# Cross-attention on one core: a new order for the first slots and for the end

## The chip, the core and the metric

The kernel runs on one core of a Trainium2 chip. A core has a matrix engine (TensorE, PE in the profile; its weight loads are listed as PEld), a vector engine (VectorE, DVE), a scalar engine (ScalarE, ACT), GpSimd (POOL) and a queue engine that mostly issues DMAs (SyncE, SP). Matmul results land in PSUM, which has eight banks of 128 x 512 floats. The metric is the device time of one execution in microseconds; lower is better.

## The reference

All inputs are fp32. `x` is 32 x 512 x 640, the context 32 x 77 x 1024. There are 20 heads of 32 columns. Only the first 77 context rows exist, so the three further attention branches of the reference have no keys and add nothing. What remains is

```python
q = heads(x @ to_q_w)                      # 32 x 20 x 512 x 32
k = heads(ctx @ to_k_w)                    # 32 x 20 x  77 x 32
v = heads(ctx @ to_v_w)
s = einsum('bhqd,bhkd->bhqk', q, k) / sqrt(32)
p = softmax(s, axis=-1)
h = merge(einsum('bhqk,bhkd->bhqd', p, v))
out = h @ to_out_w + to_out_b + x
```

## The kernel before

**Precision.** A product with weights is made of three matmuls: both operands are split into a rounded high half and the rest, and high x high, high x low and low x high are summed in PSUM (`PAIRS`). Scores and values are plain fp32 matmuls.

**First stage.** Keys and values of all 32 batches are computed from the transposed context in five groups of columns (`keys`, `values_of`) and stored to two scratch tensors in DRAM. The values of the last group (`LAST`) are not finished there: their five blocks, 24 matmuls each, are done by `context_values` next to the first attention work. After the matmuls of a block, `split_values` transposes it out of PSUM on VectorE (`vs`, L210) and GpSimd issues four stores of it (L216).

**Slots.** The rest is 160 slots, n = 5 b + j: batch b and chunk j of 128 columns, that is four heads (`HPC`) with 512 queries. Every instruction stream is in program order; there is no scheduler that reorders it. Slot n does the following, each step on its own engine:

- `scores(n)`: 16 small matmuls per query tile and head into four PSUM banks, one for each head (`sc`, four buffers). They read the query copy `qt` of this slot.
- `maxima(n)`: four reductions on VectorE, one for each bank (L430).
- `transpose_p(n - 1)`: VectorE transposes the normalized probabilities of the slot before into `z` (L459), and `move_p(n - 1)` lets four DMAs gather `z` into `raw` (L468, two buffers).
- `exps(n, i)`: ScalarE takes the exponentials of the four banks with row sums (L440); the first writes the probability tile of this slot.
- `queries(n + 1)`: 15 matmuls into the bank `pq` (L401). `copy_q(n + 1)` copies it to `qt` (L410), on VectorE as long as there is no output work, later on ScalarE.
- `values(n - 3)`: four matmuls into the bank `pa` (L478), from `raw`. `high_a` (ScalarE, L492) and `low_a` (VectorE, L497) split the result into `at`. There is one `pa` bank, so the next values wait for `low_a`.
- `normalize(n)`: a reciprocal on VectorE (L450), then GpSimd multiplies the probabilities (L452).
- `piece(...)`: 12 to 18 matmuls of an output projection (L515) of an earlier batch, in one of two output banks (`po`). `finish` adds a completed half tile to the residual tile `xr` (L544), which frees the bank, and stores the tile when both halves are there. `add_bias` adds the bias to a residual tile on GpSimd (L508).
- The x of a coming batch is loaded, transposed in four parts on VectorE (`transpose_x`, L235) and split (`split_x`, ScalarE L245 and GpSimd L246).

In slots 0 to 6 no batch is ready for its output projection (`has_out` is false). Slots 0 and 1 carry the last context blocks instead (`beside`): block 2 in slot 0, blocks 4 and 3 in slot 1. Their PSUM banks are released after slot 1 and become `pa` and the two `po` banks; from there on `po` exists, but is first used in slot 7. The values start in slot 3.

In the slots without output work the steps stand in this order, with the query copy last:

```python
        if ahead:
            queries(n + 1)
        if taken is not None and not has_out:
            values(taken)
        if len(beside) > 0:
            context_values(LAST, beside[0], psv)
        if ahead and not has_out:
            copy_q(n + 1, nc.vector.tensor_copy)
```

**End.** After slot 159, `end` finishes the projection of batch 30 (pieces 6 to 9), does the values of slots 157, 158 and 159 (`take` is values, high half, low half) and projects batch 31. By then the score banks are free, so the eight half tiles of batch 31 are begun in them and in the other banks (`begin`) and closed with the last chunk (`close`).

Of the kernel before, what the change touches and what calls it, by code (L numbers as in the profile page):

```python
# [23 lines left out]
P = 128  # L24
# [13 lines left out]
def kernel(  # L38
# [179 lines left out]
    def context_values(g, j, pool):  # L218
        values_of(g, j, pool)
        split_values(g, j)  # L220
# [12 lines left out]
    def transpose_x(b, i):  # L233
        part = xss[b][:, 4 * i : 4 * i + 4, :].rearrange("p a u -> p (a u)")
        nc.vector.transpose(part, part)  # L235
# [173 lines left out]
    def copy_q(n, copy=nc.scalar.copy):  # L409
        copy(qts[n % 2], pqs.pop(n))  # L410

    def scores(n):
        b, j = divmod(n, NC_)
        scs[n] = [ps.tile([P, NQ, P], F32, tag="sc", name="sc", bufs=4) for _ in range(HPC)]
        for t in range(NQ):
            for i, sc in enumerate(scs[n]):
                r = slice(i * HD, (i + 1) * HD)
                nc.tensor.matmul(  # L418
                    sc[:, t, :NKEY],
                    qts[n % 2][r, t * P : (t + 1) * P],  # L420
                    kbs[b % 2][r, j, :],
                    start=True,
                    stop=True,
                    tile_position=(i * HD, 0),
                )

    def maxima(n):
        nms[n] = main.tile([P, HPC, NQ], F32, tag="nm", name="nm", bufs=2)
        for i, sc in enumerate(scs[n]):
            nc.vector.tensor_reduce(  # L430
                nms[n][:, i], sc[:, :, :NKEY], AX.X, ALU.max, negate=True
            )
# [23 lines left out]
    def transpose_p(n):  # L456

        pn, z = pnb[n % 2], zs[n % 2]
        nc.vector.transpose(  # L459
            z.rearrange("p c h t j -> p (h t) c j"),  # L460
            pn.rearrange("p a (c i) -> p a c i", i=Q),
        )
# [10 lines left out]
    def values(n):  # L473
        b, j = divmod(n, NC_)
        raw, vb = raws.pop(n), vbs[b % 2][:, j]
        pas[n] = late[1].tile([P, S], F32, tag="pa", name="pa", bufs=1)
        for i in range(HPC):
            nc.tensor.matmul(  # L478
                pas[n][i * HD : (i + 1) * HD, :].rearrange("p (a q) -> p a q", q=P),
                vb[:, i, :],  # L480
                raw[:, :, i, :],
                start=True,
                stop=True,
                tile_position=(0, i * HD),
            )
# [9 lines left out]
    def low_a(n):  # L495
        at = ats[n]
        nc.vector.tensor_tensor(  # L497
            at[:, 1, :], pas.pop(n), at[:, 0, :].bitcast(F32), ALU.subtract
        )

    def load_residual(b, t, xr=None):
        if xr is None:
            xr = late[0].tile([P, C], F32, tag="xr", name="xr", bufs=4)
        nc.sync.dma_start(xr, x[b, t * P : (t + 1) * P, :])
        xrs[b, t] = xr

    def add_bias(b, t):
        nc.gpsimd.tensor_tensor(xrs[b, t], xrs[b, t], bias, ALU.add)  # L508
# [21 lines left out]
    def piece(b, i):  # L530
        for t, h, j in STEPS[CUTS[i] : CUTS[i + 1]]:
            if j == 0:
                output_bank(b, t, h)
            project(b, t, h, j)
            if j == NC_ - 1:
                closed.append((b, t, h))

    def finish():

        while closed:  # L540
            b, t, h = closed.pop(0)
            xr = xrs[b, t]
            cols = slice(h * HALF, (h + 1) * HALF)
            nc.vector.tensor_tensor(  # L544
                xr[:, cols], pos.pop((b, t, h))[:, :HALF], xr[:, cols], ALU.add
            )
            if (b, t) == (B - 1, NQ - 1):
                nc.sync.dma_start(out[b, t * P : (t + 1) * P, cols], xr[:, cols])
            elif h == 1:
                nc.sync.dma_start(out[b, t * P : (t + 1) * P, :], xr)  # L550
# [11 lines left out]
    TRANSPOSE_X = {0: (0, 1), 1: (2, 3)}  # L562
    SPLIT_X = {2: (0, 1), 3: (2, 3, 4)}

    WO = {1: (0, 1, 2), 2: (3,), 3: (4,)}
    wos = []

    def take(m):
        values(m)
        high_a(m)  # L570
        low_a(m)

    def slot(n, beside=()):
        b, j = divmod(n, NC_)
        ahead, more = n + 1 < N, b + 1 < B
        back, first = PIECES[j]
        bo_, has_out = b - back, b >= back
        xsplits = (SPLIT_X if b else {0: (2,), 1: (3,), 2: (4,)}).get(j, ()) if more else ()
        turns = TRANSPOSE_X.get(j, ()) if more and b else ()
        if b == 1 and j < 2:  # L580
            turns = ((), range(NQ))[j]
        taken = takes.get(n)
        scores(n)
        if taken is not None and has_out:
            values(taken)
        maxima(n)
        if n:
            transpose_p(n - 1)
        for k in WO.get(n, ()):
            nc.sync.dma_start(wos[0][:, k].bitcast(F32), wo_dram[:, k].bitcast(F32))  # L590
        if j == 0 and more:
            load_keys(b + 1)
        if j == 1:
            load_values(b)
        if b + 2 < B:
            quarters = {4: (0, 1), 5: (2, 3)}.get(n, ()) if n <= NC_ else (j - 1,) if j else ()
            if quarters:
                load_x(2 if n <= NC_ else b + 2, quarters)
        if j in RESIDUAL and b >= RESIDUAL[j][0]:
            load_residual(b - RESIDUAL[j][0], RESIDUAL[j][1])  # L600
        if j in BIAS and b >= BIAS[j][0]:
            add_bias(b - BIAS[j][0], BIAS[j][1])
        if has_out:
            piece(bo_, first)
        for i in range(2):
            exps(n, i)
        finish()
        if n >= LATE:
            move_p(n - 1)
        for i in turns:  # L610
            transpose_x(b + 1, i)
        if len(beside) > 1:
            context_values(LAST, beside[1], psv)
        if ahead:
            queries(n + 1)
        if taken is not None and not has_out:
            values(taken)
        if len(beside) > 0:
            context_values(LAST, beside[0], psv)
        if ahead and not has_out:  # L620
            copy_q(n + 1, nc.vector.tensor_copy)
        for i in range(2, HPC):
            exps(n, i)
        normalize(n)
        if taken is not None:
            high_a(taken)
        if has_out and ahead:
            copy_q(n + 1)
        if has_out:
            piece(bo_, first + 1)  # L630
        if taken is not None:
            low_a(taken)
        for c in xsplits:
            split_x(b + 1, c)
        finish()

    def end():


        last = B - 1  # L640
        transpose_p(N - 1)
        add_bias(last - 1, 3)
        piece(last - 1, 6)
        finish()
        load_residual(last, 0)
        load_residual(last, 1)
        piece(last - 1, 7)
        finish()
        move_p(N - 1)
        take(N - 3)  # L650
        piece(last - 1, 8)
        piece(last - 1, 9)
        finish()
        load_residual(last, 2)

        def begin(i, j0, j1):
            t, h = divmod(i, 2)
            if j0 == 0:
                if i < 4:
                    pos[last, t, h] = ps.tile([P, S], F32, tag="sc", name="po", bufs=4)  # L660
                elif i == 4:
                    pos[last, t, h] = ps.tile([P, S], F32, tag="pq", name="po", bufs=1)
                elif i < 7:
                    output_bank(last, t, h)
                else:
                    pos[last, t, h] = late[1].tile([P, S], F32, tag="pa", name="po", bufs=1)
            for j in range(j0, j1):
                project(last, t, h, j)

        for i in range(2):  # L670
            begin(i, 0, 2)
        take(N - 2)
        for t in (0, 1, 2):
            add_bias(last, t)
        for i in range(2, 5):
            begin(i, 0, 3)
        for i in range(2):
            begin(i, 2, 4)
        for i in range(2, 5):
            begin(i, 3, 4)  # L680
        take(N - 1)
        load_residual(last, 3)
        add_bias(last, 3)
        begin(5, 0, 4)

        def close(t):
            for h in range(2):
                project(last, t, h, 4)
                closed.append((last, t, h))
            finish()  # L690

        close(0)
        close(1)
        begin(6, 0, 4)
        close(2)
        begin(7, 0, 4)
        close(3)
# [65 lines left out]
```

## Time and profile before

| | us |
|---|---|
| median of 3 runs | 1775.46 |
| lowest and highest run | 1770.51 and 1776.66 |
| profiled execution, its own time | 1775.36 |
| span of the profiled execution | 1773.6 |
| TensorE busy (share of the span) | 1757.1 (99%) |
| ScalarE busy | 1110.5 (63%) |
| VectorE busy | 976.5 (55%) |
| GpSimd busy | 787.4 (44%) |
| mean granted clock of TensorE | 0.995 |

The span runs from the first to the last instruction of the profiled execution; its own time holds 1.8 us more. Rows of a timeline give start, duration, engine, line, operation, tiles and the number of merged instructions, and in brackets the idle time before the first of them with what ended it. That releaser is inferred, so where two instructions of the same engine end close together, it can be the neighbour of the true one. A query by stretches gives the busy time of each engine in a stretch, the clock that TensorE was granted (1.00 is full), the share of time in which the DMA engines were busy, and their rate.

### The profile page before, as it was taken

The page shows a single profiled execution, that of the slowest core. Times are in us where ns is not written, and L with a number is a line of the kernel's source. Part 1 is how long each engine was busy: PE and PEld are TensorE (multiplying, and loading weights), DVE is VectorE, ACT ScalarE, POOL GpSimd, SP SyncE. Part 2 cuts the span into 40 slices and gives each one's busy share as a digit, 9 for nine tenths or more (in the row PEclk, how much of TensorE's full clock was granted, in tenths as well). Part 3 has the DMA queues.
Part 4 walks back from the last instruction along what each step waited for, and adds up shares of the span by engine and source line. Part 5 has one row for each costly group of instructions (what it writes and reads, how often), then busy time and mean ns, then how long its engine had stood idle before and what let it go on. Part 6 is the DMA issues. An engine that isn't in the chain of part 4 may idle for free.

```text
span 1773.6 us, 39529 instructions
## 1 busy us (share of the span) xinstructions
PE 1757.1 (99%) x13862; PEld 1431.8 (81%) x13862; DVE 976.5 (55%) x1651; ACT 1110.5 (63%) x5698; POOL 787.4 (44%) x502
## 2 busy tenths in 40 slices
PE   9999998999999999999999999999999999999998
PEld 7888897788878888888888888888888888888887
DVE  5333134566655666556665566555665556665553
ACT  3132125777767777777777777777776777776761
POOL 0000035545544455444555545555555554454442
PEclk9999999999999999999999999999999999999999
DMA  9846556877777777767777777777777777677654
GB/s 186 159 93 179 107 118 172 198 180 177 189 178 181 179 179 189 187 176 179 183 180 181 181 184 180 177 184 179 180 179 186 189 185 180 181 181 186 156 144 135
DMA packets 268566, 306.60 MB, mean 173 GB/s; under 512 B 88720, under 2 KB 165008, under 8 KB 268368
## 3 DMA queue, kind: packets, MB, share of 16 engines
q1 hardware_dynamic: 265776, 296.94, 68.6%
q0 software_dynamic: 2496, 6.97, 1.4%
q8 instruction: 110, 1.80, 0.4%
q14 instruction: 88, 0.72, 0.1%
q10 hardware_dynamic: 96, 0.16, 0.0%
HBM read 120.27 MB, written 57.88 MB: 100 GB/s over the span
## 4 chain that ended last, share of the span: by engine, by line
PE 95%; ACT 2%; DVE 1%; POOL 1%; issue 0%; DMA 0%; SPq 0%; DVEq 0%; POOLq 0%; ACTq 0%
PE po L515 33%; PE pq L401 30%; PE sc L418 9%; PE pa L478 9%; PE pv L177 7%; PE pk L177 7%; ACT pn L440 2%; POOL pn L452 1%; POOL xr L508 0%; DMA cs<-in_ctx_dram 0%; DVE nm L430 0%; DVE xs L235 0%; DVE z L459 0%; DVE qt L410 0%; SPq L145 0%
## 5 line engine op out<-in xcount | busy, mean ns | idle before, releaser
L440 ACT ACTIVATE pn<-sc,nm 128x77 f32<-128x77 f32 x2560 | 789.0, 362 | 377.5 <-DVE nm L430 288.9
L515 PEld LDWEIGHTS po<-wo_s,at 128*128 128x128 f32 x3840 | 578.6, 189 | 148.8 <-issue 132.5
L452 POOL TENSOR_TENSOR pn<-pn,rs 128x1232 f32<-128x1232 f32 x160 | 364.5, 2278 | 710.3 <-DVE rs L450 703.4
L515 PE MATMUL po<-wo_s,at 128*128 128x320 f32 x3840 | 632.4, 314 | 3.2 <-DVE xr L544 3.2
L440 ACT ACTIVATION_READ_ACCUMULATOR pn<-sc,nm 128x1 f32 x2560 | 621.2, 243 | 0.0
L401 PE MATMUL pq<-xt,wq_s 128*128 128x512 f32 x1680 | 414.1, 393 | 0.0
L430 DVE TENSOR_REDUCE nm<-sc 128x4 f32<-128x308 f32 x640 | 261.3, 470 | 244.0 <-PE sc L418 244.0
L401 PEld LDWEIGHTS pq<-xt,wq_s 128*128 128x128 f32 x1680 | 309.9, 188 | 58.2
L459 DVE STREAM_TRANSPOSE z<-pn 128x1536 f32<-128x1536 f32 x160 | 282.8, 1768 | 4.9 <-POOL pn L452 4.9
L508 POOL TENSOR_TENSOR xr<-xr,bias 128x640 f32<-128x640 f32 x128 | 200.0, 1563 | 10.9 <-DMA xr<-in_x_dram 10.9
L418 PEld LDWEIGHTS sc<-kb,qt 32*128 32x128 f32 x5120 | 158.9, 187 | 42.1 <-issue 29.7
L418 PE MATMUL sc<-kb,qt 32*128 32x77 f32 x5120 | 183.0, 278 | 7.6 <-DVE rs L450 5.1
L401 PE MATMUL pq<-xu,wq_s 128*128 128x512 f32 x720 | 180.6, 394 | 0.0
L478 PE MATMUL pa<-raw,vb 96*32 96x512 f32 x1280 | 172.2, 610 | 0.0
L544 DVE TENSOR_TENSOR xr<-po,xr 128x320 f32<-128x320 f32 x256 | 117.4, 469 | 96.2 <-PE po L515 94.4
L401 PEld LDWEIGHTS pq<-xu,wq_s 128*128 128x128 f32 x720 | 134.9, 187 | 32.4
L450 DVE RECIPROCAL rs<-sm 128x16 f32<-128x16 f32 x160 | 40.4, 253 | 213.0 <-ACT pn L440 213.0
L246 POOL TENSOR_TENSOR xt<-xs,xt 128x512 fp32r<-128x512 f32 x112 | 140.0, 1275 | 36.9 <-ACT xt L245 36.9
L497 DVE TENSOR_TENSOR at<-pa,at 128x512 fp32r<-128x512 f32 x160 | 110.6, 691 | 49.5 <-ACT at L492 49.5
L177 PE MATMUL pk<-ct,wk_s 128*128 128x512 f32 (+1 forms) x600 | 133.5, 381 | 0.5 <-ACT wk_s L89 0.3
L177 PE MATMUL pv<-ct,wv_s 128*128 128x512 f32 (+1 forms) x600 | 133.9, 381 | 0.0
L177 PEld LDWEIGHTS pk<-ct,wk_s 128*128 128x128 f32 x600 | 112.3, 188 | 20.0 <-ACT wk_s L89 0.8
(35 smaller groups left out, 796.0 us busy)
## 6 DMA issues: line engine op xcount, KB each, us to landing
raw<-z SPq DMA_DIRECT2D x640, 192.0 KB, 3.4
xs<-in_x_dram SPq DMA_DIRECT2D x128, 320.0 KB, 4.9
xr<-in_x_dram SPq DMA_DIRECT2D x128, 320.0 KB, 4.8
out_dram<-xr SPq DMA_DIRECT2D x127, 320.0 KB, 2.2
vb<-v_dram SPq DMA_DIRECT2D x32, 240.0 KB, 3.7
kb<-k_dram SPq DMA_DIRECT2D x32, 192.5 KB, 3.8
cs<-in_ctx_dram SPq DMA_DIRECT2D x12, 512.0 KB, 9.4
k_dram<-ks POOLq DMA_DIRECT2D x20, 256.0 KB, 2.7
```

Of the source, the lines that this page charges most:

```text
L177: nc.tensor.matmul(held[j][:, :gn], w[:, k, a, :], cts[g, k][:, c, :gn], start=(k == 0 and n == 0), stop=(k == NK - 1 and n == 2),)
L246: low.tensor_tensor(parts[1], src, parts[0].bitcast(F32), ALU.subtract)
L401: nc.tensor.matmul(pqs[n], wq_s[:, k, a, j * P : (j + 1) * P], xts[b, k][:, c, :], start=(k == 0 and m == 0), stop=(k == NC_ - 1 and m == 2),)
L418: nc.tensor.matmul(sc[:, t, :NKEY], qts[n % 2][r, t * P : (t + 1) * P], kbs[b % 2][r, j, :], start=True, stop=True, tile_position=(i * HD, 0),
L430: nc.vector.tensor_reduce(nms[n][:, i], sc[:, :, :NKEY], AX.X, ALU.max, negate=True)
L440: nc.scalar.activation(pnb[n % 2][:, at, :NKEY], sc[:, t, :NKEY], AF.Exp, bias=nms[n][:, i, t : t + 1], accum_out=sms[n][:, at : at + 1],)
L452: nc.gpsimd.tensor_tensor(pf, pf, rs.unsqueeze(2).to_broadcast([P, NQ * HPC, NKEY]), ALU.mult)
L459: nc.vector.transpose(z.rearrange("p c h t j -> p (h t) c j"), pn.rearrange("p a (c i) -> p a c i", i=Q),)
L478: nc.tensor.matmul(pas[n][i * HD : (i + 1) * HD, :].rearrange("p (a q) -> p a q", q=P), vb[:, i, :], raw[:, :, i, :], start=True, stop=Tru ...
L508: nc.gpsimd.tensor_tensor(xrs[b, t], xrs[b, t], bias, ALU.add)
L515: nc.tensor.matmul(pos[b, t, h][:, :HALF], ats[b * NC_ + j][:, a, t * P : (t + 1) * P], wos[0][:, j, c, h * HALF : (h + 1) * HALF], start= ...
L544: nc.vector.tensor_tensor(xr[:, cols], pos.pop((b, t, h))[:, :HALF], xr[:, cols], ALU.add)
```

## The change

It has two parts. In the slots without output work, the query copy moves directly behind the queries, ahead of values, context block and x transpositions. The low half of the values of slots 0 to 2 (taken in slots 3 to 5) is held back and issued behind the maxima of the next slot. The four x transpositions of slot 6 are shared between slots 6 and 7. The scores of slots 3, 4 and 6 put two of their four tiles in the two output banks. At the end, the bias of the last tile of batch 30 is added in slot 159 ahead of its normalization; the values of slot 157 come ahead of pieces 7 to 9 and the transposition of the last probabilities, and the first addition follows the low half of slot 156 directly; the other values and the projections of batch 31 follow in a new order.

```diff
     def scores(n):
         b, j = divmod(n, NC_)
-        scs[n] = [ps.tile([P, NQ, P], F32, tag="sc", name="sc", bufs=4) for _ in range(HPC)]
+        scs[n] = [
+            late[1].tile([P, NQ, P], F32, tag="po", name="sc", bufs=2)
+            if i in LENT.get(n, ())
+            else ps.tile([P, NQ, P], F32, tag="sc", name="sc", bufs=4)
+            for i in range(HPC)
+        ]
...
+    LENT = {3: (0, 1), 4: (2, 3), 6: (0, 1)}
+    held = []
...
-        if b == 1 and j < 2:
-            turns = ((), range(NQ))[j]
+        if b == 1 and j < 3:
+            turns = ((), (0, 1), (2, 3))[j]
...
         maxima(n)
+        while held:
+            low_a(held.pop())
         if n:
             transpose_p(n - 1)
...
+        if n == N - 1:
+            add_bias(b - 1, 3)
         if has_out:
             piece(bo_, first)
...
-        for i in turns:
-            transpose_x(b + 1, i)
+        if has_out:
+            for i in turns:
+                transpose_x(b + 1, i)
         if len(beside) > 1:
             context_values(LAST, beside[1], psv)
         if ahead:
             queries(n + 1)
-        if taken is not None and not has_out:
-            values(taken)
-        if len(beside) > 0:
-            context_values(LAST, beside[0], psv)
-        if ahead and not has_out:
+        if not has_out:
             copy_q(n + 1, nc.vector.tensor_copy)
+            if taken is not None:
+                values(taken)
+            if beside:
+                context_values(LAST, beside[0], psv)
+            for i in turns:
+                transpose_x(b + 1, i)
...
-        if taken is not None:
+        if taken is not None and n < NC_ + 1:
+            held.append(taken)
+        elif taken is not None:
             low_a(taken)
...
-        transpose_p(N - 1)
-        add_bias(last - 1, 3)
         piece(last - 1, 6)
+        values(N - 3)
+        high_a(N - 3)
         finish()
+        low_a(N - 3)
         load_residual(last, 0)
         load_residual(last, 1)
         piece(last - 1, 7)
         finish()
+        transpose_p(N - 1)
         move_p(N - 1)
-        take(N - 3)
         piece(last - 1, 8)
+        finish()
+        take(N - 2)
         piece(last - 1, 9)
         finish()
         load_residual(last, 2)
+        for t in (0, 1, 2):
+            add_bias(last, t)
...
-        for i in range(2):
-            begin(i, 0, 2)
-        take(N - 2)
-        for t in (0, 1, 2):
-            add_bias(last, t)
-        for i in range(2, 5):
-            begin(i, 0, 3)
-        for i in range(2):
-            begin(i, 2, 4)
-        for i in range(2, 5):
-            begin(i, 3, 4)
+        for i in range(4):
+            begin(i, 0, 4)
         take(N - 1)
         load_residual(last, 3)
         add_bias(last, 3)
-        begin(5, 0, 4)
+        for i in (4, 5):
+            begin(i, 0, 4)
```

## The prediction

> **What bounds the kernel now.** I read the page first, then TensorE's groups and its timeline in the two places that the change touches, and last the granted clock there.
>
> ```profile
> span 1773.6 us, 39529 instructions
> PE 1757.1 (99%) x13862; PEld 1431.8 (81%) x13862; DVE 976.5 (55%) x1651; ACT 1110.5 (63%) x5698; POOL 787.4 (44%) x502
> ...
> raw<-z SPq DMA_DIRECT2D x640, 192.0 KB, 3.4
> ...
> xr<-in_x_dram SPq DMA_DIRECT2D x128, 320.0 KB, 4.8
> ```
>
> TensorE is busy for 99%. No matmul is added or removed, so a gain can only come from its holes and from matmuls that run slowly. The groups say which line has holes: scores 7.6 us in all, 1.7 of it in three waits for exponentials.
>
> ```profile
> L418 PE MATMUL sc<-kb,qt 32*128 32x77 f32 x5120 | 183.0, 278 | 7.6 <-DVE rs L450 5.1 <-ACT pn L440 1.7 <-ACT xu L245 0.9
> ```
>
> TensorE's timeline (start, duration, instructions, and in brackets the idle time before them) shows them in slots 1 to 7. The last five rows are an undisturbed slot.
>
> ```profile
> 273.08 1.13 PE L418 MATMUL sc<-kb,qt 32*128 32x77 f32 x32 [1.38 <-DVE rs L450]
> ...
> 282.15 4.69 PE L177 MATMUL pv<-ct,wv_s 128*128 128x416 f32 x24
> 288.21 1.13 PE L418 MATMUL sc<-kb,qt 32*128 32x77 f32 x32 [1.38 <-DVE rs L450]
> 289.27 5.28 PE L401 MATMUL pq<-xt,wq_s 128*128 128x512 f32 x15
> 295.43 1.13 PE L418 MATMUL sc<-kb,qt 32*128 32x77 f32 x32 [0.87 <-ACT xu L245]
> ...
> 323.68 1.91 PE L418 MATMUL sc<-kb,qt 32*128 32x77 f32 x32 [2.30 <-DVE rs L450]
> ...
> 330.72 1.55 PE L401 MATMUL pq<-xt,wq_s 128*128 128x512 f32 x6
> ...
> 336.06 1.13 PE L418 MATMUL sc<-kb,qt 32*128 32x77 f32 x32
> ...
> 349.24 3.60 PE L401 MATMUL pq<-xt,wq_s 128*128 128x512 f32 x15
> 352.68 1.92 PE L515 MATMUL po<-wo_s,at 128*128 128x320 f32 x12
> 354.53 1.13 PE L418 MATMUL sc<-kb,qt 32*128 32x77 f32 x32
> 355.59 1.06 PE L478 MATMUL pa<-raw,vb 96*32 96x512 f32 x8
> 356.58 0.70 PE L515 MATMUL po<-wo_s,at 128*128 128x320 f32 x3
> ```
>
> From start to start, undisturbed queries cost 3.44 us, 12 projections 1.85, scores 1.06, values 0.99; a context block of 24 costs 4.69. From the scores of slot 1 (273.08) to those of slot 8 (336.06) there are 7 scores, 2 context blocks, 7 queries, 5 values and 24 projections: 7.42 + 9.38 + 24.08 + 4.95 + 3.70 = 49.5 us of work in 62.98. So 13.5 us are lost, and 1.4 just before: 14.9, twice the idle time. The rest is the clock (columns: PE busy, granted clock, DMA share, GB/s):
>
> ```profile
> 273.10:289.70 16.60, 15.22 (x129) 1.00 0.56 173
> 289.70:289.80 0.10, 0.10 (x2) 0.54 0.61 123
> 293.10:293.20 0.10, 0.10 (x2) 0.90 0.51 164
> 323.80:323.90 0.10, 0.10 (x8) 0.71 0.94 353
> 330.60:330.70 0.10, 0.10 (x2) 0.66 0.89 184
> 303.00:317.00 14.00, 12.96 (x118) 1.00 1.00 213
> ```
>
> After the 1.38 us hole before 288.21 the clock halves at about 289.75 and returns at 293.16, 3.41 us later; after the 2.30 us hole it halves at 323.84 and returns at 330.66, two such windows. The price is half the cold time: 1.7 or 3.4 us. Slots 4 and 5, with holes of about 0.6 us (1.7 over three), stay at 1.00, and so does the stretch after the other hole of 1.38 us, the one before 273.08.
>
> The second place is the end:
>
> ```profile
> 1731.67 6.43 PE L515 MATMUL po<-wo_s,at 128*128 128x320 f32 x42
> 1741.30 1.97 PE L515 MATMUL po<-wo_s,at 128*128 128x320 f32 x6 [3.21 <-DVE xr L544]
> ...
> 1751.49 1.06 PE L478 MATMUL pa<-raw,vb 96*32 96x512 f32 x8
> ```
>
> 3.21 us idle, and then 42 projections and one values take 10.19 us instead of 42 x 0.154 + 0.99 = 7.46: another 2.73. Together 5.9 us. All that is to be had is 14.9 + 5.9 = 20.8 us.
>
> **Fill, slots 0 and 1: query copy ahead of the context block.**
>
> ```profile
> 286.87 0.62 DVE L210 STREAM_TRANSPOSE vs<-pv 128x416 f32<-128x416 f32 x1 [7.06 <-PE pv L177]
> ...
> 292.67 1.78 DVE L459 STREAM_TRANSPOSE z<-pn 128x1536 f32<-128x1536 f32 x1 [1.70 <-POOL pn L452]
> 294.59 0.69 DVE L410 COPY qt<-pq 128x512 f32<-128x512 f32 x1
> ...
> 303.26 1.62 DVE L430 TENSOR_REDUCE nm<-sc 128x4 f32<-128x308 f32 x4
> ...
> 309.35 0.69 DVE L497 TENSOR_TENSOR at<-pa,at 128x512 fp32r<-128x512 f32 x1 [0.22 <-ACT at L492]
> 309.95 1.62 DVE L430 TENSOR_REDUCE nm<-sc 128x4 f32<-128x308 f32 x4
> ...
> 319.98 2.98 DVE L235 STREAM_TRANSPOSE xs<-xs 128x640 f32<-128x640 f32 x4
> ```
>
> The wait is put down to the reciprocal, but what the scores read is the copy, which stands behind the transposition of the values, and that waits for the whole context block. Moved ahead, the copy runs while TensorE multiplies. Both 1.38 us holes go: scores of slot 1 at 271.7, of slot 2 at 271.7 + (286.84 - 273.08) = 285.5 instead of 288.2. Gain so far 2.7 us, and the cold window after 289.75 has lost its cause.
>
> **What is late next: the scores of slot 3.** Queries now end at 285.5 + 1.06 + 3.44 = 290.0. But their copy stays behind the z transposition on VectorE, and that behind GpSimd:
>
> ```profile
> 287.79 2.55 POOL L216 DMA_DIRECT2D v_dram<-vs  x4 [5.09 <-DVE vs L210]
> 290.35 2.29 POOL L452 TENSOR_TENSOR pn<-pn,rs 128x1232 f32<-128x1232 f32 x1
> ```
>
> GpSimd still issues the four value stores (2.55 us) before the normalization (2.29), then z (1.78) and the copy (0.69). This chain starts with the last context block and only moves with it, by 1.4 us: scores of slot 3 at 295.43 - 1.4 = 294.0. A hole of 4.0 us opens where TensorE had been working slowly. Lent banks do not help here, since the copy is last. A hole of 4.0 us is longer than both that halved the clock, so I charge a cold time: 1.7 (one window) to 3.4 us (two), 2.4 taken as about the middle, for where the window falls in the hole is chance.
>
> By the Trainium skill ("TensorE: Matmul & The Clock Gate", Part 1) the activity window is 3413 ns, free-running, and the clock drops after at least one idle window; the trace agrees on the 3.41 us, but here a hole of 1.38 us was enough. By the page's rule the fill would lose no cold time unless the hole covered a whole window, and the charge of 2.4 would mostly fall away.
>
> **Slots 3 to 6: lent banks, and the subtraction behind the maxima.** Scores of slot 4: 294.0 + 1.06 + 3.44 + 0.99 + 2.4 = 301.9. Then the period. Before it is 309.95 - 303.26 = 6.69 us, a ring: exponentials, high half, low half, maxima, exponentials. With the low half behind the maxima, its 0.60 us and the 0.22 us wait for ScalarE leave the ring: 5.87. The lent banks take the 0.6 us bank wait away, so that scores are there when the maxima can start. Queued behind the held subtraction are z and the query copy, and the values wait for its bank; it ends about 2.3 us after the maxima begin (1.62 + 0.69), values come 4.5 after the scores begin: covered by the queries. Three slots of 5.9: scores of slot 7 at 319.6.
>
> **Slots 6 and 7: x transpositions.** Before, four of them (2.98 us) held up the query copy: the 2.30 us hole, and the cold stretch in which 323.68 to 330.72 took 7.04 us for 3.90 of work. Now the copy goes first, and two of four lie in each slot. New in slot 7: all four of its scores use the ordinary banks, the last of which is still being read (0.6 us, as the three waits before), and its values wait for the low half, which now stands behind two transpositions (1.49 us); an estimate of 0.6 remains open. Slot 7 takes 1.06 + 0.99 + 1.85 + 3.44 + 1.85 + 1.2 = 10.4. Scores of slot 8 at 330.0 instead of 336.06: fill gains **6.0 us**. Bounds: 6.7 with one cold window, 5.0 with two; 14.9 if nothing were lost.
>
> **The end.**
>
> ```profile
> 1736.87 0.69 DVE L497 TENSOR_TENSOR at<-pa,at 128x512 fp32r<-128x512 f32 x1 [0.22 <-ACT at L492]
> 1739.09 1.78 DVE L459 STREAM_TRANSPOSE z<-pn 128x1536 f32<-128x1536 f32 x1 [1.54 <-POOL pn L452]
> 1740.80 0.85 DVE L544 TENSOR_TENSOR xr<-po,xr 128x320 f32<-128x320 f32 x2
> ```
>
> ```profile
> 1734.99 2.62 SPq L468 DMA_DIRECT2D raw<-z  x4
> ```
>
> The hole came from the two additions behind z: they free the output banks. Now one addition directly follows the low half of 156 (ended 1737.56), so its bank is free at about 1738. TensorE does 36 projections (1731.67 + 5.54 = 1737.2), then values(157), which wait for the same low half, 0.5 us; then 24 projections meet free banks. z(159) moves behind the low half of 157, from 1739.1 to about 1740.4. Its four moves, 2.6 us of issue and 3.4 of landing, are done near 1748; values(159) come after 12 + 48 projections and values(158), at about 1752.5. The bias addition moved ahead of the last normalization waits for a load issued in slot 159, 4.8 us; normalization has 1.3 us of slack, since z waits for the low half anyway. The first addition of the last batch runs when its operands are long there. Stores and the tail after the last projection stay. Gain 5.9 - 0.5 = **5.4 us**; bounds 4.5 (another 0.9 of waiting) to 5.9.
>
> **Sum.** 6.0 + 5.4 = 11.4. The profiled execution took 1775.36 us around its span of 1773.6, within 0.1 of the median of 1775.46: 1775.36 - 11.4 = **1764.0 us**.
>
> **Rivals.**
> 1. *Slot 7 halves the clock too.* Its waits (0.6 + 0.6, and a short one for the copy) sum to about 1.3 us, near the 1.38 that was enough once and not enough once. Price 1.7 to 3.4, taken 2.5: 1766.5.
> 2. *The clock stays up in the 4.0 us hole*, as the page's rule would mostly have it: 2.4 less, of which the chain absorbs a little: 1762. Against it: 1.38 us dropped it.
> 3. *The fill is limited by transfers.* The DMA share is 1.00 in slots 4 and 5, with four moves of 192 KB a slot; if they cannot be packed closer, slots 3 to 7 keep their times and only the end gains: 1770. Against it: TensorE waits for no transfer before, and the moves have nearly two slots to land.
> 4. *Slower: every short hole in slots 4 to 7 trips the gate.* Each costs up to 3.4, 13.6 in all: 1764.0 + 13.6 = 1777.6. It decides if holes of about 0.6 us suffice; the row of 303 to 317 with clock 1.00 speaks against it.
>
> **How the numbers follow.** A measurement of this kernel can tell about 0.5%, 8.9 us, from no change: faster is below 1766.6, slower above 1784.3, which no case reaches by itself. Forecast 0.55, rivals 0.2, 0.07, 0.13, 0.03, rest 0.02. Rival 1 lies on the boundary, half and half; the forecast and rival 2 are faster, less 0.08 since the runs before spread by 6 us. Faster 0.64, same 0.34, slower 0.02. Range: from rival 2 less 2 us of that spread, 1760.0, to rival 3, 1770.0.
>
> **What would show it.** Right: no idle time before the scores of slots 1 and 2; about 4 us before those of slot 3, released by VectorE, and a clock of 0.50 after it; maxima every 5.9 us in slots 4 to 6; scores of slot 8 near 330; no 3.2 us hole near 1738 and a clock of 1.00 to the end. Wrong: values waiting for moves, a clock of 0.50 in slot 7, or scores of slot 3 that start as soon as their queries end.

## The result: 0.4% faster, most of the fill's gain gone in slot 7

| | us |
|---|---|
| before, median of 6 runs | 1773.46 (1770.51 to 1776.66) |
| after, median of 6 runs | 1766.64 (1764.64 to 1768.73) |
| ratio, with 95% interval | 0.9960 (0.9947 to 0.9974) |
| forecast | 1764.0 (1760.0 to 1770.0) |
| after, profiled execution and its span | 1768.15 and 1766.4 |

The time lies in the range, 2.6 us above the forecast, and the change of 0.4% is below what was called faster. The gain is further off than the time: of the forecast's 11.4 us the medians show 6.8, and the profiled executions 7.2: 1775.36 less 1768.15. The forecast was counted from 1775.36, the median of the kernel before is 1773.46 with all six runs, and these 1.9 us brought the time nearer to the forecast by chance. TensorE's waits in the changed kernel (line, tile, releaser, us in total, times, longest) show two of note:

```profile
PE sc L423 <- DVE qt L410: 3.9, 2, 3.6
PE pa L483 <- DMA raw<-z: 1.7, 1, 1.7
```

The first is the forecast hole before the scores of slot 3. The second was not in the sum: values that wait for the moves that gather their probabilities. TensorE's timeline of the changed kernel (start, duration, instructions, idle time before in brackets) shows both in place:

```profile
271.62 1.13 PE L423 MATMUL sc<-kb,qt 32*128 32x77 f32 x32
...
285.31 1.13 PE L423 MATMUL sc<-kb,qt 32*128 32x77 f32 x32
...
293.61 2.00 PE L423 MATMUL sc<-kb,qt 32*128 32x77 f32 x32 [3.56 <-DVE qt L410]
...
301.77 1.13 PE L423 MATMUL sc<-kb,qt 32*128 32x77 f32 x32
...
319.51 0.46 PE L423 MATMUL sc<-kb,qt 32*128 32x77 f32 x6
320.50 1.11 PE L423 MATMUL sc<-kb,qt 32*128 32x77 f32 x26 [0.54 <-ACT pn L445]
323.36 1.93 PE L483 MATMUL pa<-raw,vb 96*32 96x512 f32 x8 [1.74 <-DMA raw<-z]
325.22 3.57 PE L520 MATMUL po<-wo_s,at 128*128 128x320 f32 x12
...
334.48 1.13 PE L423 MATMUL sc<-kb,qt 32*128 32x77 f32 x32
```

At the scores of slot 7 the new kernel is 4.2 us ahead of the old (319.51 against 323.68); at those of slot 8 only 1.6 (334.48 against 336.06). Slot 7 takes 14.97 us for 9.19 of work: 1.05 in the scores around the bank wait, 1.74 in the wait for the moves, and 2.99 in what follows, where 12 projections take 3.57 us instead of about 2. That is the clock (columns: PE busy, granted clock, DMA share, GB/s):

```profile
292.20:292.30 0.10, 0.00 (x0) 0.56 0.67 143
299.00:299.10 0.10, 0.10 (x2) 0.80 1.19 307
322.80:323.00 0.20, 0.00 (x0) 0.83 0.97 198
323.00:329.00 6.00, 5.64 (x21) 0.50 1.09 236
329.70:329.80 0.10, 0.10 (x1) 0.71 0.94 251
1728.00:1766.00 38.00, 34.16 (x257) 1.00 0.52 155
```

The mixed values mark the edges: the clock is halved from about 292.21 to 299.04 and from about 322.93 to 329.76, two windows of 3.4 us each time. At the end it is 1.00 throughout, and there the hole is gone but for 0.43 us:

```profile
1728.03 1.13 PE L423 MATMUL sc<-kb,qt 32*128 32x77 f32 x32
1729.09 1.06 PE L483 MATMUL pa<-raw,vb 96*32 96x512 f32 x8
1730.09 5.55 PE L520 MATMUL po<-wo_s,at 128*128 128x320 f32 x36
1736.07 1.07 PE L483 MATMUL pa<-raw,vb 96*32 96x512 f32 x8 [0.43 <-issue]
```

Scores of slot 159 stood at 1729.61 before. 1.58 of the 7.2 us come from the fill, the other 5.6 from the end.

Why the moves are late is in the moves of slot 4's probabilities, which the values of slot 7 read. Their rows in the view of the tile `raw`, first before, then after (issue times from the first to the last of four, and the time from issue to landing):

```profile
L468 SPq DMA_DIRECT2D raw<-z x4: 591/597/650, 314.7 to 316.7; - x4
...
DMA to landing us min/median/max: 4.3/4.5/4.7
```

```profile
L473 SPq DMA_DIRECT2D raw<-z x4: 592/599/806, 313.4 to 315.4; - x4
...
DMA to landing us min/median/max: 6.9/7.2/7.9
```

They are issued 1.3 us earlier and land later: the last of them by 316.7 + 4.7 = 321.4 before, and by 315.4 + 7.9 = 323.3 after, which is when the values start. What stands ahead of them is in the values of slot 5 and in the queue engine's timeline of the changed kernel:

```profile
312.32 1.07 PE L483 MATMUL pa<-raw,vb 96*32 96x512 f32 x8
```

```profile
310.23 1.68 SPq L387 DMA_DIRECT2D kb<-k_dram  x1
311.95 1.16 SPq L231 DMA_DIRECT2D xs<-in_x_dram  x2
313.45 2.73 SPq L473 DMA_DIRECT2D raw<-z  x4
```

A load of keys and two of x are issued in the 3.2 us before the moves. Before, the same loads were issued in the 3.4 us ahead of these moves, but the slots were longer: 6.69 us against 5.79 and 6.15. The moves start 0.06 us after the values of slot 5 end (312.32 + 1.07 = 313.39), since there are two `raw` buffers and these values free one: the date of issue hangs on the values two slots earlier. The chain of work that ended last runs the same way, from these values through the issues and 7.85 us of landing to the values of slot 7. In slots 3 to 6 the values stand behind the queries; from slot 7 on they follow the scores directly and need the moves one query stage earlier.

### The profile page after: what moved, and what is told of

It is laid out like the page before. It is cut to its first block, busy times and chain, and to the rows that moved or that the text cites. A ratio compares the mean times of both kernels' runs of the same rounds, so it can differ in the third digit from the quotient of the medians.

```text
span 1766.4 us, 39534 instructions
## 1 busy us (share of the span) xinstructions
PE 1753.7 (99%) x13862; PEld 1430.6 (81%) x13862; DVE 976.2 (55%) x1651; ACT 1109.7 (63%) x5698; POOL 787.5 (45%) x502
## 4 chain that ended last, share of the span: by engine, by line
PE 98%; DMA 1%; issue 0%; SPq 0%; POOL 0%; DVE 0%; ACT 0%; DVEq 0%; ACTq 0%
PE po L520 34%; PE pq L401 31%; PE sc L423 9%; PE pa L483 9%; PE pv L177 7%; PE pk L177 7%; DMA raw<-z 1%; DMA wraw<-in_L_xattn_to_k_w_dram 0%; POOL pn L457 0%; SPq L145 0%; SPq L473 0%; DVE wk_s L90 0%; ACT wk_s L89 0%; SPq L99 0%; DVE qt L410 0%
## 5 line engine op out<-in xcount | busy, mean ns | idle before, releaser
L410 ACT COPY qt<-pq 128x512 f32<-128x512 f32 x153 | 93.5, 611 | 58.4 <-PE pq L401 58.4
```

## Experiments

Each kernel has four to nine runs, beside runs of the kernel before on the same chip. There were three sets, each on a chip of its own: rows 1 to 4, 5 to 8 and 9 to 12, with 1775.06, 1773.86 and 1774.06 us for the kernel before. Across sets the ratio is the better comparison, and ratios whose intervals overlap are not told apart by it.

| kernel | median us | ratio to before (95%) |
|---|---|---|
| fill only | 1769.92 | 0.9974 (0.9964 to 0.9983) |
| end only | 1770.14 | 0.9971 (0.9959 to 0.9982) |
| x loads one slot earlier | 1764.39 | 0.9938 (0.9926 to 0.9951) |
| copy of slot 2 ahead of z | 1768.42 | 0.9965 (0.9953 to 0.9977) |
| the changed kernel again | 1765.53 | 0.9956 (0.9942 to 0.9969) |
| copy ahead, x loads in slot 1 | 1759.77 | 0.9930 (0.9916 to 0.9943) |
| no lent banks | 1765.27 | 0.9958 (0.9944 to 0.9972) |
| low half not held | 1767.76 | 0.9967 (0.9954 to 0.9980) |
| before, one line of the end moved | 1769.14 | 0.9971 (0.9960 to 0.9982) |
| copy ahead, x loads in slot 1, that one line | 1759.36 | 0.9918 (0.9905 to 0.9932) |
| the same fill, no lent banks | 1762.16 | 0.9930 (0.9918 to 0.9943) |
| x loads earlier, TensorE kept warm | 1765.46 | 0.9949 (0.9936 to 0.9961) |

The theory: the fill's gain is lost in slot 7, to moves that queue behind other transfers, and the hole then halves the clock. Rivals: the hole before slot 3 is the loss; the lent banks or the held low half don't bring what they should; the end brought less than its trace shows.

**The two parts alone.** One kernel has the new fill with the old end, the other the old fill with the new end.

> The fill part of the change alone, the end as before. By the traces (scores of slot 8 at 334.48 after against 336.06 before) the fill gives only 1.6 us in the profiled execution, with a clock at half speed in slot 3 and slot 7: about 1.5 to 3 us under the kernel before, near 1771. By the prediction's term it would give 6.0: near 1767.5. The clock of 0.50 and the wait of the values of slot 7 for their moves should be there as in the changed kernel.

> The end part of the change alone, the fill as before. Theory: the end gives 5.4 to 5.6 us whatever the fill does, since slots 8 to 158 are the same: about 1768 against 1773.5. Rival: the two parts are not independent and the end gives under 4. In the profile: no idle 3.2 us before projections, a clock of 1.00 from slot 159 on, about 0.4 us of idle before the values of slot 157.

Each brings about 0.3%; for the fill this is more than the 1.5 to 3 us expected of it. Fill only has a slot 7 of 13.15 us (scores at 319.65 and 332.80, values after 1.28 us of idle time) and keeps the 3.2 us hole of the end; end only has no hole there and a fill as before. The profiled execution of fill only took 5.9 us less than that of the kernel before, but only 3.26 of them are there at the scores of slot 8. The rest is the clock at the end, which did not fall after the hole (before 1738.04; columns as above):

```profile
1738.00:1739.00 1.00, 0.96 (x6) 1.00 0.62 246
```

From the scores of slot 159 its end took 37.5 us to the last projections, with the same instructions 40.2 in the kernel before. The two parts add to 0.55% where both together measured 0.40 and, in a second set, 0.44%. The intervals overlap, and part of the remainder may be this clock: where it stays up by itself, the new end has less to gain.

**x loads one slot earlier.** The quarters of x of the third batch (four loads of 320 KB), which go through the same queue as the moves, are issued in slots 3 and 4.

```diff
-            quarters = {4: (0, 1), 5: (2, 3)}.get(n, ()) if n <= NC_ else (j - 1,) if j else ()
+            quarters = {3: (0, 1), 4: (2, 3)}.get(n, ()) if n <= NC_ else (j - 1,) if j else ()
```

> The changed kernel with the four x loads of slots 4 and 5 issued one slot earlier, where the DMA engines were idle for 3 us (300 to 303). Theory (transfers): the values of slot 7 waited 1.7 us because their four moves stood behind keys and x loads and took 7.2 us to land instead of 3.4; with the loads out of the way they land in under 6, the wait goes or falls under 0.5 us, and the clock falls in slot 7 in fewer executions: 2 to 4.5 us less than the changed kernel, 1762 to 1764.5. Rival (VectorE): the values wait for the low half behind the two x transpositions anyway, then they start at most 0.3 us earlier and the time stays at 1766.6.

1764.39, at the slow end of the 1762 to 1764.5 expected: 1.1 to 2.3 us below the changed kernel, whose medians are 1766.64 and 1765.53 in other sets, with overlapping intervals. The profiled execution is the fastest of its five (1762.27). TensorE's timeline in slot 7:

```profile
318.20 0.46 PE L423 MATMUL sc<-kb,qt 32*128 32x77 f32 x6
319.20 1.11 PE L423 MATMUL sc<-kb,qt 32*128 32x77 f32 x26 [0.54 <-ACT pn L445]
320.40 1.06 PE L483 MATMUL pa<-raw,vb 96*32 96x512 f32 x8
...
328.61 0.57 PE L423 MATMUL sc<-kb,qt 32*128 32x77 f32 x12
```

The values wait for no move (landing 5.1 us instead of 7.2), the clock stays at 1.00, and the slot takes 10.41 us, which is the forecast's 10.4. The bank wait of 0.54 is still there, and by itself it halved nothing here.

**Query copy of slot 2 ahead of z.** This removes the hole before the scores of slot 3.

```diff
-        if n:
+        if n and n not in COPY_FIRST:       # COPY_FIRST = (2,)
             transpose_p(n - 1)
...
-        if n >= LATE:
+        if n >= LATE and n not in COPY_FIRST:
             move_p(n - 1)
...
             copy_q(n + 1, nc.vector.tensor_copy)
+            if n in COPY_FIRST:
+                transpose_p(n - 1)
+                move_p(n - 1)
```

> The changed kernel with the z transposition of slot 2 (and its moves) behind the query copy instead of ahead of it. Theory (chain through GpSimd): the scores of slot 3 start near 291 instead of 293.6, idle time before them is under 1.0 us instead of 3.6, the clock stays at 1.00 there, and slot 4 begins 5 us earlier; of that 3 us are left at slot 8, as the ring of slots 4 to 6 takes its 5.9 a slot: 1763 to 1764. Rival (transfers decide slot 7): the moves land no earlier, what was gained is waited for before the values of slot 7, and the time stays within 1 us of the changed kernel.

1768.42, no better. TensorE's timeline of this kernel:

```profile
316.66 1.59 PE L423 MATMUL sc<-kb,qt 32*128 32x77 f32 x32 [0.48 <-DVE qt L410]
323.67 1.94 PE L483 MATMUL pa<-raw,vb 96*32 96x512 f32 x8 [5.42 <-DVE nm L435]
...
334.16 1.02 PE L423 MATMUL sc<-kb,qt 32*128 32x77 f32 x28
```

The scores of slot 7 are 2.85 us earlier than in the changed kernel, those of slot 8 only 0.3: nearly all of it is waited away. The releaser is inferred as a reduction, but the moves that these values read say otherwise:

```profile
L473 SPq DMA_DIRECT2D raw<-z x4: 591/599/875, 310.9 to 313.1; - x4
...
DMA to landing us min/median/max: 9.7/10.3/10.5
```

The last of them lands by 313.1 + 10.5 = 323.6: issued 2.5 us earlier than in the changed kernel, they land at nearly the same time. In the changed kernel the hole before slot 3 thus has next to no cost of its own: transfers set the next date.

**Both.** If transfers and hole limit in turn, taking both away must give more than the two alone. The copy is ahead as above, and all four quarters are loaded in slot 1, three to four slots earlier than in the changed kernel, where the experiment above moved them by one.

```diff
-            quarters = {4: (0, 1), 5: (2, 3)}.get(n, ()) if n <= NC_ else (j - 1,) if j else ()
+            quarters = {1: range(4)}.get(n, ()) if n <= NC_ else (j - 1,) if j else ()
```

> The changed kernel with the query copy of slot 2 ahead of the z transposition and all four loads of the third x in slot 1. Theory (two limits in turn, the chain in slot 2 and the transfers before slot 7): each alone left the other standing; together the scores of slot 3 start near 291 with the clock at 1.00, the values of slot 7 wait under 0.5 us, and the scores of slot 8 start near 326 instead of 334.5: 6 to 8 us less than the changed kernel, 1759 to 1761, and 2 to 4 less than with the early loads alone. Rival (the loads only move the congestion to the moves of slots 1 to 3): the moves of the first slots land late, TensorE waits for them in slots 3 to 5, and the time is 1764 or more.

1759.77. TensorE's timeline, and the clock over the whole stretch:

```profile
297.78 1.13 PE L423 MATMUL sc<-kb,qt 32*128 32x77 f32 x32 [1.48 <-DVE qt L410]
...
325.89 1.13 PE L423 MATMUL sc<-kb,qt 32*128 32x77 f32 x32
```

```profile
289.00:326.00 37.00, 33.73 (x307) 1.00 0.91 219
```

The moves of slot 4 land in 3.3 us (3.8 at most), no values wait for them, the clock is never halved, and the scores of slot 8 stand at 325.89, 8.6 us ahead of the changed kernel. From the scores of slot 4 to those of slot 8 this takes 28.11 us, and 28.14 with the loads one slot earlier (300.47 to 328.61): the whole difference of 2.7 us between these two lies ahead of slot 4, where the copy was moved. Loads in slot 1 without the moved copy were not tried.

**The changed kernel again**, on the chip of "both" and of the next two kernels.

> The changed kernel once more, on the chip of the three kernels below. If the two parts add up as measured alone (0.26% and 0.29%), about 0.5% under the kernel before; if the fill's gain is partly the phase of the clock windows, 0.35 to 0.45%.

1765.53, or 0.44%. In its profiled execution the wait for the moves is 0.65 us and slot 7 takes 12.54, so the loss in slot 7 varies from one execution to the next: 5.8 us in one, 3.35 in the other.

**No lent banks** (`LENT = {}`).

> The changed kernel with all scores in their own four banks. The period of slots 4 to 6 should be 6.7 us instead of 5.8 (the scores wait for the last exponentials), and the scores of slot 7 start 1.5 to 2.7 us later. Theory (transfers set slot 7): the moves land at nearly the same time as in the changed kernel, the 1.7 us wait for them shrinks by as much, and the time is within 1.5 us of the changed kernel. Rival (the ring sets the fill, as the prediction had it): the whole 2.7 us are lost.

1765.27, the same as with them. Without them the maxima come every 6.6 us, so the scores of slot 7 start at 321.49 instead of 319.51; but the moves have landed by then, and slot 8 starts at 331.79. Their last one lands by 317.0 + 6.5 = 323.5, nearly when it does in the changed kernel (323.3). What the banks gain, the wait for the moves and the half clock behind it take.

**Low half not held** (ahead of the maxima again, `n < NC_ + 1` replaced by `n < 0`).

> The changed kernel with the low half of the values ahead of the maxima again, banks lent as in the change. Ring of exponentials, high half, low half, maxima: period of slots 4 to 6 6.5 to 6.7 us instead of 5.8, scores of slot 7 about 2 us later. Theory (transfers): of this under 1.5 us are left at slot 8. Rival (ring): all of it is left.

1767.76, which is 2.2 us more than the changed kernel in the same set, though the intervals of the ratios overlap. VectorE's timeline shows the maxima of this kernel at the period of before; the changed kernel stands below it:

```profile
303.11 1.62 DVE L435 TENSOR_REDUCE nm<-sc 128x4 f32<-128x308 f32 x4
309.80 1.62 DVE L435 TENSOR_REDUCE nm<-sc 128x4 f32<-128x308 f32 x4
```

```profile
302.92 1.64 DVE L435 TENSOR_REDUCE nm<-sc 128x4 f32<-128x308 f32 x4 [1.19 <-PE sc L423]
...
308.71 1.61 DVE L435 TENSOR_REDUCE nm<-sc 128x4 f32<-128x308 f32 x4
...
314.86 1.63 DVE L435 TENSOR_REDUCE nm<-sc 128x4 f32<-128x308 f32 x4 [0.31 <-PE sc L423]
```

6.69 us against 5.79 and 6.15: the ring is as it was reckoned. In the profiled execution, the slowest of the five, the scores of slot 7 are 1.1 us later than in the changed kernel's first profile (320.62 against 319.51) and those of slot 8 only 0.3 (334.77 against 334.48), which speaks for the transfers. The median speaks against: its 2.2 us are more than the 1.5 that this theory allowed, so what the held half is worth stays open.

**One line of the end.** The kernel before, with the transposition of the last probabilities moved behind the addition that it held up.

```diff
-        transpose_p(N - 1)
         add_bias(last - 1, 3)
         piece(last - 1, 6)
         finish()
+        transpose_p(N - 1)
```

> The kernel before with one line moved: the transposition of the last probabilities behind the first addition of the end; everything else, the fill too, as before. Theory (the addition stood behind that transposition, nothing else in the new end matters): the idle 3.2 us and the half-speed clock at the end go, 5 to 6 us less than the kernel before, at least what the whole new end gives alone (0.29%). Rival (the values of slot 157 ahead of the last pieces are needed too): another wait of over 1 us appears in the last 40 us and the gain is under 3.5 us.

1769.14, 0.29% as with the whole new end. TensorE's timeline of its end has no idle time at all:

```profile
1729.34 1.13 PE L418 MATMUL sc<-kb,qt 32*128 32x77 f32 x32
...
1731.39 7.47 PE L515 MATMUL po<-wo_s,at 128*128 128x320 f32 x48
1738.79 1.07 PE L478 MATMUL pa<-raw,vb 96*32 96x512 f32 x8
```

From the scores of slot 159 to the end of the last projections it takes 34.2 us, the changed kernel 34.6, the kernel before 40.2. The other moves of the new end add nothing that these runs show.

**The best fill with that end.** The fill of "both", and the end of before with the one line moved.

> The changed kernel with the query copy of slot 2 first and the x loads in slot 1, and with the end of the kernel before but for that one moved line. If the one move is enough, within 1 us of the kernel with the whole new end (1759.8), perhaps 0.4 below it, as the values of slot 157 no longer wait for the low half before them. If the new order of the end matters, 1.5 us or more above it.

1759.36, ratio 0.9918, the lowest median of the kernels run: 14.7 us below before (not told apart from "both"). The times of this kernel and of "both" fall in two groups, 1759.1 to 1759.8 and 1762.5 to 1762.7. The profiled execution of this one is from the upper group, and its windows show why:

```profile
300.00:302.00 2.00, 2.00 (x6) 0.50 1.02 265
...
321.00:323.00 2.00, 2.00 (x11) 0.50 1.03 256
```

```profile
298.18 1.13 PE L423 MATMUL sc<-kb,qt 32*128 32x77 f32 x32 [1.44 <-DVE qt L410]
```

The scores of slot 4 with the hole ahead of them, in its timeline, are the second row. A hole of 1.44 us is followed by a halved clock here; in "both" one of 1.48 us at the same place was not. Its clock is halved for one window after this hole and for another from about 320, where only short holes stand ahead of it: 0.38 and 0.39 us of idle time before scores and values of slot 7, and a short bank wait between them. Two windows at half clock cost 2 x 1.7 = 3.4 us, an estimate near the distance of the groups.

**The same fill without lent banks** ("both" with `LENT = {}`).

> The kernel with both edits, but all scores in their own four banks. In the changed kernel that made no difference. Theory (there it was hidden by transfers and by the clock): here neither is late, the period of slots 4 to 6 is 6.7 instead of 5.9, and 2 to 3 us are lost: 1762 to 1763. Rival (the lent banks are worth nothing): within 0.7 us of 1759.8.

1762.16, against 1759.77 with them, in another set. Its intervals overlap too, but the profiled execution shows two bank waits within the scores of slot 3, and queries at half clock behind them:

```profile
290.61 0.45 PE L423 MATMUL sc<-kb,qt 32*128 32x77 f32 x6 [0.88 <-ACT pn L445]
291.78 1.80 PE L423 MATMUL sc<-kb,qt 32*128 32x77 f32 x26 [0.72 <-ACT pn L445]
293.51 6.15 PE L401 MATMUL pq<-xt,wq_s 128*128 128x512 f32 x15
```

Of the 4.05 us by which its scores of slot 8 are later than in "both" (329.94 against 325.89), 2.75 lie in slot 3, with these waits and this clock, and 1.4 in the longer period of the slots behind. The execution is the slowest of the five. So the lent banks seem to pay once neither transfers nor the hole hide them, more by slot 3 than by the period that was expected to cost.

**TensorE kept warm in the hole.** x loads one slot earlier, and 14 matmuls that nobody reads, after the query copy of slot 2.

```diff
+            if n == 2:
+                idle = late[1].tile([P, S], F32, tag="pa", name="pa", bufs=1)
+                for _ in range(14):
+                    nc.tensor.matmul(idle, wq_s[:, 0, 0, :P], xts[1, 0][:, 0, :], start=True, stop=True)
```

> The changed kernel with the early x loads and with 14 matmuls that nobody reads put into the hole before the scores of slot 3, about 3.2 of its 3.6 us. The scores of slot 3 start at the same time or up to 0.3 us later. Theory (the clock charge): the clock stays at 1.00 in slot 3, scores and queries there take 4.7 us instead of 6.4 to 7.3, and 1.5 to 2.5 us are gained: 1762 to 1763. Rival (the hole costs only its own length): no gain, 1764.4 or more.

1765.46: no gain over 1764.39 (in another set), a miss. TensorE's timeline shows both halves of it:

```profile
293.28 1.13 PE L423 MATMUL sc<-kb,qt 32*128 32x77 f32 x32 [0.39 <-DVE qt L410]
...
298.96 1.13 PE L423 MATMUL sc<-kb,qt 32*128 32x77 f32 x32
...
311.92 1.06 PE L483 MATMUL pa<-raw,vb 96*32 96x512 f32 x8 [1.84 <-DMA raw<-z]
314.31 1.13 PE L423 MATMUL sc<-kb,qt 32*128 32x77 f32 x32 [1.32 <-DVE rs L455]
```

The clock stays up, and the scores of slot 4 come 1.5 us earlier (298.96 against 300.47). Then values wait 1.84 us for moves again, two slots sooner than in the changed kernel, and the clock halves there. These moves were issued from 299.1 and took up to 10.7 us: once slot 4 starts earlier, loads one slot earlier are not early enough.

## Why the prediction was right or wrong

- **Slots 0 to 2: right.** Forecast 271.7 and 285.5, measured 271.62 and 285.31.
- **The hole before slot 3: right.** Forecast 294.0 with 4.0 us of idle time and 2.4 of cold time, released by the query copy behind z; measured 293.61, 3.56 and 2.67 (7.17 us from these scores to the next values, 4.50 undisturbed). Rival 2, the clock staying up, fell in this execution; over the same hole of 3.56 us the second profile of this kernel shows one half-clock window only, of 3.41 us.
- **Slots 3 to 6: right.** Slot 4 at 301.77 for 301.9, a period of 5.79 and 6.15 for 5.9, slot 7 at 319.51 for 319.6. With the low half back ahead of the maxima the period is 6.69.
- **Slot 7: the step that failed.** "Slot 7 takes 1.06 + 0.99 + 1.85 + 3.44 + 1.85 + 1.2 = 10.4": it took 14.97 (12.54 in the other execution, 13.15 with the fill alone). Of the 1.2, the bank wait was 1.05 instead of 0.6 and the low half cost nothing that can be seen. What the term lacked is 1.74 us for the moves and 2.99 of half clock. The argument that failed stands under rival 3: "TensorE waits for no transfer before, and the moves have nearly two slots to land". Idle time of zero gave no slack: before, the last move landed by 321.4 and was needed at 325.5, when slot 7's values started; the forecast itself needed it at 319.6 + 1.06 + 0.6 = 321.3. The slots became shorter and the bytes remained. With the x loads one slot earlier the slot takes 10.41. In the five profiles with a wait there (the changed kernel twice, fill only, copy of slot 2 ahead, low half not held) the values of slot 7 start 0.06 to 0.2 us after the last move has landed, reckoned as its issue plus the longest landing.
- **The end: right.** Forecast 5.4, measured 5.6. That the addition behind z was the cause is shown by the one moved line. But 2.73 of the forecast's 5.9 us at the end are half clock, and in fill only the same hole brought none: this half of the price depends on the execution.
- **The rivals.** What happened is rival 1's half clock in slot 7, by rival 3's mechanism in that one slot. Its 1766.5 against the measured 1766.64 is luck: it charged 2.5 us for slot 7, which lost 4.6, and 1.9 came back with the lower time of the kernel before. Rival 4 fell for slots 4 to 6 of the changed kernel, where a hole of 0.36 us was followed by no halved clock. But short holes are not harmless: in slot 7 of the best kernel's profile three of them within 2.5 us were followed by a half-clock window. In "both", where holes of 0.38 and 0.54 us lie over 6 us apart, none followed.
- **The sum.** 6.0 + 5.4 was forecast, 1.6 + 5.6 came in the profiled executions; of the 4.2 that are missing slot 7 alone cost 4.6, and the other steps together came out 0.4 better. Over 0.5% faster, held the likeliest outcome, did not come. One reading was off without effect: the rows put the first half-clock window before the change at 289.71 to 293.12, not 289.75 to 293.16.

Not tried by itself: the other moves of the new end one by one, the x loads in slot 1 without the moved copy, and a third buffer for the moves. In the changed kernel the probabilities of slot 4 are transposed by 311.25 + 1.78 = 313.03, so a third buffer could have brought the issue at 313.45 forward by 0.4 us at most. Whether the moves are late because they stand behind the loads in one queue, or because they share the DMA engines with them, these runs do not tell.

## What to carry to other kernels

When a stage is packed closer, list for every transfer on which it depends when it lands now and when it will be needed, and do not take it that an earlier issue lands earlier: zero idle time before says nothing of the slack. Where two limits stand in a row (here a hole, then late transfers), taking away the first alone gave nothing, and both together gave more than the second alone (1759.77 against 1764.39 by median, though the loads were moved further and the intervals of the ratios overlap); test the pair before a part is dropped. At each hole ask what stands on the releasing engine ahead of the needed instruction: at the end of this kernel one moved line gave all that the whole new order gave.

## What the runs showed of the hardware

Moves between on-chip buffers that were issued 2.5 us earlier landed at nearly the same time (7.2 us to landing became 10.3), while the DMA engines' busy share was 1.14 (310 to 324 us of that kernel; 0.82 from 309 to 316 in the kernel whose x loads lie in slot 1); with the x loads taken out of their way they landed in 3.3. The share alone does not tell the landing: in the kernel before it was 1.11 from 314.7 to 321.4, and the moves took 4.5. And the clock falls differently from run to run: the same instructions of the old end left a hole of 3.21 us and a half clock of 6.8 us, begun within it, in the kernel before, and a hole of 3.20 us with no half clock in the one with the fill only. In the best fill, holes of 1.44 and 1.48 us at the same place were followed by one half-clock window in one execution and by none in another, and its times lie in two groups 3 us apart. By the Trainium skill ("TensorE: Matmul & The Clock Gate", Part 1) the windows run freely, so that the same kernel differs from run to run, and the clock drops after at least one idle window of about 3.4 us. The first agrees with these differences; the second doesn't, since the hole of 1.44 us was enough.
